# Cross-attention over 8192 context rows: feature-major context, statistics and factors through DRAM, keys and values kept in DRAM, units of 16 chunks

## The chip, the cores and the metric

The kernel runs on one core of a Trainium2 chip. The time is the device time in microseconds of one launch. The engines are PE (TensorE), DVE (VectorE), ACT (ScalarE), POOL (GpSimd) and SP (SyncE, which here only issues DMAs); each works through its own instructions in order, and semaphores tie them together. All arithmetic is in 32-bit floats.

## What is computed

A block of a perceiver: cross-attention of 512 latent tokens over 8192 context rows plus the latents themselves, then eight layers of a linear-attention transformer, then a layer of expert-choice feed-forward. The change touches the first part alone:

```
xn = layer_norm(ctx, gamma_x, beta_x)          # 8192 x 512
ln = layer_norm(latents, gamma_l, beta_l)      # 512 x 512
q  = (ln @ Wq) * 64**-0.5                      # 8 heads of 64
k_x, v_x = split(xn @ Wkv);  k_l, v_l = split(ln @ Wkv)
k_x = rope_rotate(k_x)
k, v = concat([k_x, k_l]), concat([v_x, v_l])  # 8704 rows
out = softmax(q k^T) v @ Wo
x   = x + out
```

## The kernel before

Context rows come in 16 blocks of 512 (numbers 1 to 16; block 0 holds the latents), a block in 4 chunks of 128 rows: 68 chunks in all. The eight heads form four pairs p.

**Preparing a block.** `fetch_block` loads four row tiles (128 rows x 512 features each) and the rotation table `trig`. `moments_of` takes mean and variance of each row on DVE, `roots_of` the reciprocal root on POOL for blocks after 2 (a chain of small instructions with Newton steps), `centre` subtracts and scales the rows on ACT, in place. `transpose_rows` then turns the block on PE, 16 transposes of 128x128 through PSUM, and ACT applies gamma and beta per feature on the way back (`xT`, four tiles [feature, row]). `keys_of` multiplies `xT` with Wkv for one of four groups of output features, DVE multiplies with cosine and sine, POOL adds the two halves, and eight DMAs of 64 KB on SP's queue bring the result of two groups into key tiles `k_sb[b, p]` [2 heads x 64, 512 rows] in SBUF. `values_of` gives 128 rows x 512 features, which ACT copies out of PSUM in four parts into `v_sb[b, p]`. All key and value tiles stay in SBUF until used: 27 buffers.

**Attention in units.** A unit is one pair over a run of chunks; units go round the pairs, and the number of chunks that a unit reaches grows with the blocks that are ready (`STEP = 3.25`, most units 13 chunks, 24 units). For each chunk `score` makes two 128x512 products into PSUM (five banks, `ps_s`, shared with keys, values, transposes and small helpers), ACT copies them to `sc`, and DVE keeps a running maximum `mx`. At a unit's end `maxima` transposes the running maximum on PE, reduces it on DVE to `mrow`, and forms the factor `alpha` = exp(old - new), the difference on POOL and the exponential on ACT. `maxima_rows` spreads `mrow` over PSUM (`mbc`). Then `exponentials` (DVE subtracts `mbc`, ACT takes the exponential, POOL adds into `es`) and `weigh` (PE, with the values, into `po`) run for this unit while the next unit's scores are made. `shrink` spreads `alpha` along rows by 16 small PE products into `pa` and multiplies the accumulated output `oT[p]` on DVE; `gather` adds `po` and the sum of exponentials `pd`.

**What sets the order.** The work is put into numbered steps (`at(step, function, ...)`). Each step makes the scores of two chunks and then does what is due in it, by `rank`. Block b begins at step 8(b-2); its pieces (four of keys, four of values) follow one per step, and the normalizing of block b+1 is spread over the same eight steps by `normalizing`, where the number is the offset. PE keeps the order of the code; the other engines' order is made by a scheduler when the kernel is built, with hints (`queued`, `tc.issue_after`) that hold an instruction behind another. SP issues nearly all DMAs, in one order.

Of the kernel before, what the change touches and what calls it, by code (L numbers as in the profile page):

```python
# [8 lines left out]
F32 = mybir.dt.float32  # L9
# [7 lines left out]
P = 128  # L17
# [37 lines left out]
def perceiver_kernel(  # L55
    ctx: ExitStack, tc: tile.TileContext, x, cx, wq_x, wkv_x, wo_x, wq, wk, wv, wo, wf1, wf2,
# [81 lines left out]
    xnp = pool("x_feat", 4, stack=xa)  # L138
    cbp = pool("x_rows", 4, stack=xa)
    xpool = pool("xattn", 1, stack=xa)  # L140
    kvp = pool("x_kv", 27, stack=xa)
    sp = pool("x_s", 18, stack=xa)
# [5 lines left out]
    def rows_tile(name):  # L148
        return cbp.tile([P, D], F32, tag="rows", name=name)
# [29 lines left out]
    def roots_of(b):  # L179
        eng = nc.gpsimd if b > 2 else nc.vector  # L180
        with queued(behind):
            r = rsqrt_of(mvs[b][:, :, 1], TT, 1e-5, eng)
        n = small.tile([P, TT], F32, tag="nmr", name="nmr")
        stt(eng, n, mvs[b][:, :, 0], -1.0, r, ALU.mult, ALU.mult)
        roots[b] = r, n

# [9 lines left out]
    def normalizing(b):  # L196

        yield from ((1 + t // 2, moments_of, b, t) for t in range(TT))
        yield (3, roots_of, b)
        yield from ((6 + t // 2, centre, b, t) for t in range(TT))  # L200
# [11 lines left out]
    k_sb, v_sb, xT, part, rows_of, trigs = {}, {}, {}, {}, {}, {}  # L212
# [13 lines left out]
    def keys_of(b, j):  # L226
# [21 lines left out]
        for p in (j - 1, j):  # L248
            k_sb[b, p] = kv_tile(f"k{b}_{p}")
            for h in range(2):  # L250
                src = slice((p % 2 * 2 + h) * H2, (p % 2 * 2 + h + 1) * H2)
                for i, half_of in enumerate((lo, hi)):
                    o = h * HD + i * H2
                    nc.sync.dma_start(out=k_sb[b, p][o : o + H2, :], in_=half_of[src, :])

    def values_of(b, t):
# [5 lines left out]
        for p in range(NPAIR):  # L262
            if t == 0:
                v_sb[b, p] = kv_tile(f"v{b}_{p}")
            nc.scalar.copy(v_sb[b, p][:, t * P : (t + 1) * P], pv[:, p * P : (p + 1) * P])  # L265
# [4 lines left out]
    def fetch_block(b):  # L270
        rows_of[b] = [rows_tile(f"cb{t}") for t in range(TT)]
        load_rows(
            rows_of[b], cx[(b - 1) * BLK : b * BLK, :], (nc.sync, nc.scalar) if b == 1 else (nc.sync,)
        )
        if b == 1:
            with tc.issue_after(loaded[0].ins):
                nc.scalar.dma_start(out=col, in_=cols)
            fetch_weights(0)
        trigs[b] = xpool.tile([P, 2, BLK], F32, tag="trig", name="tg", bufs=1)
# [6 lines left out]
    def fetch_last():  # L286
        wo_last.extend(rows_tile(f"wo{p}") for p in range(NPAIR))
# [20 lines left out]
    fetch_block(2)  # L308
    normalize_block(0)
# [19 lines left out]
    STEP = 3.25  # L329
    units, met, k = [], [0] * NPAIR, 0  # L330
    while min(met) < NCHUNK:
        p = k % NPAIR
        upto = min(NCHUNK, int(3 + STEP * k)) if k else 4
# [16 lines left out]
    for b in range(2, NBLK + 1):  # L350
        begin, gap = 8 * (b - 2), 1 if b < NBLK else 2

        for dc in range(DC):
            if dc == 2 and b > 2:
                at(begin, values_of, b - 1, TT - 1)
            at(begin, transpose_rows, b, dc, C_GX, C_BX)
        at(begin, *((fetch_block, b + 1) if b < NBLK else (fetch_last,)))
        pieces = *((keys_of, j) for j in range(2)), (values_of, 0), *((keys_of, j) for j in (2, 3)), (values_of, 1), (values_of, 2)
        for j, (f, i) in enumerate(pieces, 1):
# [3 lines left out]
    at(begin + 8 * gap, values_of, NBLK, TT - 1)  # L363
    pieced = set(todo)

    scores, mx, mrow, alpha, mbc, es, po = {}, {}, {}, {}, {}, {}, {}

    def score(u, i):
# [3 lines left out]
        for h in range(2):  # L372
            hs = slice(h * HD, (h + 1) * HD)
            nc.tensor.matmul(pc[h], k_sb[b, p][hs, o : o + P], qT[hs, p, :], start=True, stop=True)  # L374
# [10 lines left out]
    def maxima(u):  # L385
# [13 lines left out]
        if p in mrow:  # L399
            a = alpha[u] = small.tile([P, 2 * TT], F32, tag="alpha", name="alpha", bufs=4)  # L400
            nc.gpsimd.tensor_tensor(a, mrow[p], new, ALU.subtract)
            nc.scalar.activation(a, a, AF.Exp)
        mrow[p] = new
# [11 lines left out]
    def shrink(u):  # L415

        p = units[u][0]
        pa = bank("pa")
        for qc in range(TT):
            for h in range(2):  # L420
                c = h * TT + qc
                nc.tensor.matmul(
                    pa[h * HD : (h + 1) * HD, qc * P : (qc + 1) * P],
                    alpha[u][:, c : c + 1].to_broadcast([P, HD]), ident,
                    start=True, stop=True,
                )
# [948 lines left out]
```

## Time and profile before

| | us |
|---|---|
| median of 3 runs | 2578.23 (2577.60 to 2579.33) |
| the profiled execution, span | 2575.6 |
| PE busy in the stretch 100 to 1100 | 981 of 1000 |
| ACT, exponentials (L435) x272 | 288.3 |
| ACT, copies of scores (L377) x544 | 284.3 |
| DVE, subtraction of the maximum (L434) x272 | 319.7 |
| DVE, running maximum (L383) x448 | 283.4 |
| POOL, sums of exponentials (L445) x222 | 525.3 |

Attention runs from the first scores, at 85.5 us, to about 1236 us; the layers behind it fill the rest of the span. Some rows of the groups, with line, engine, operation, tiles, shapes and count, then the busy time in us, the mean of one in ns, and the idle time of the engine just before them with what ended it:

```profile
L246 POOL TENSOR_TENSOR cos<-cos,sin 128x512 f32<-128x512 f32 x32 | 40.9, 1280 | 0.0
L194 ACT ACTIVATE cb<-cb,nmr,ny 128x512 f32<-128x512 f32 x62 | 47.8, 838 | 4.0 <-DVE nmr L82 4.0
L224 ACT ACTIVATE xn<-pt,col 128x512 f32<-128x512 f32 x66 | 49.3, 795 | 14.0 <-PE pv L259 11.9 <-PE pt L218 1.7
L265 ACT COPY v<-pv 128x128 f32<-128x128 f32 x272 | 51.5, 275 | 37.0 <-PE pv L259 37.0
```

And from the list of DMA issues, with size and the median time from issue to landing:

```profile
k<-cos SPq DMA_DIRECT2D x272, 64.0 KB, 2.0
cb<-in_cx SPq DMA_DIRECT2D x62, 256.0 KB, 3.4
tg<-in_trig SPq DMA_DIRECT2D x16, 512.0 KB, 3.8
```

### The profile page before, as it was taken

To read this page: it belongs to the slowest core of one execution; us is meant where nothing else is said; L and a number is where in the kernel's file an instruction comes from. 1 tells how busy PE (TensorE), PEld (TensorE's weight loads), DVE (VectorE), ACT (ScalarE), POOL (GpSimd) and SP (SyncE) were. 2 spreads that over 40 slices of the span, in tenths; PEclk is the share of its full clock that TensorE was granted. 3 is DMA by queue.
4 is the path that set the end of the run, shared out by engine and by line. 5 is a ranking of instruction groups with operands and counts; after the bars stand their busy time and mean duration, and the time that the engine had idled before them with its cause. 6 is when DMAs were issued, how large, how long until landed. Compare 5 with 4: busy or idle time off the path is not lost.

```text
span 2575.6 us, 32550 instructions
## 1 busy us (share of the span) xinstructions
PE 2514.4 (98%) x10984; PEld 1490.5 (58%) x10984; DVE 1747.0 (68%) x3680; ACT 1202.9 (47%) x2285; POOL 1263.1 (49%) x1422
## 2 busy tenths in 40 slices
PE   8999999999999999997999999999999999999998
PEld 4434333334343343333588686886868868687764
DVE  4466777766677776886675766757676575766764
ACT  2465666665566666663443415334153441524303
POOL 0255665666567666675054352444525354263512
PEclk9999999999999999998999999999999999999999
DMA  4111011111111111010522223222222222222236
GB/s 136 39 45 52 27 41 42 41 41 41 33 42 41 42 41 41 9 41 17 192 94 81 84 69 116 95 94 70 95 91 94 94 86 96 93 74 98 66 113 199
DMA packets 98375, 187.41 MB, mean 73 GB/s; under 512 B 10336, under 2 KB 10464, under 8 KB 98208
## 3 DMA queue, kind: packets, MB, share of 16 engines
q1 hardware_dynamic: 88496, 167.29, 20.0%
q10 hardware_dynamic: 8688, 15.94, 1.9%
q0 software_dynamic: 1024, 2.10, 0.3%
q8 instruction: 87, 1.43, 0.2%
q14 instruction: 80, 0.66, 0.1%
HBM read 162.22 MB, written 1.05 MB: 63 GB/s over the span
## 4 chain that ended last, share of the span: by engine, by line
PE 80%; DVE 9%; ACT 5%; issue 4%; POOL 2%; DMA 0%; POOLq 0%; DVEq 0%; ACTq 0%
PE pb L839 14%; PE ps L628 13%; PE pw L723 9%; PE pv L259 7%; PE po L455 7%; PE pk L230 6%; PE pc L374 6%; PE ps L723 6%; PE po L1002 4%; DVE sc L434 4%; ACT sc L377 2%; ACT sc L435 1%; POOL es L445 1%; PE pt L218 1%; PE pf L932 1%
## 5 line engine op out<-in xcount | busy, mean ns | idle before, releaser
L445 POOL TENSOR_TENSOR es<-es,sc 128x1024 f32<-128x1024 f32 x222 | 525.3, 2366 | 111.0 <-ACT sc L435 99.9
L383 DVE TENSOR_TENSOR mx<-pc,mx 128x512 f32<-128x512 f32 x448 | 283.4, 685 | 190.7 <-ACT sc L377 190.5
L435 ACT ACTIVATE sc<-sc 128x1024 f32<-128x1024 f32 x272 | 288.3, 1064 | 242.8 <-DVE sc L434 231.7
L377 ACT COPY sc<-pc 128x512 f32<-128x512 f32 x544 | 284.3, 599 | 91.4 <-PE pc L374 78.8
L434 DVE TENSOR_TENSOR sc<-sc,mbc 128x1024 f32<-128x1024 f32 x272 | 319.7, 1211 | 3.7 <-PE mbc L411 2.2
L374 PE MATMUL pc<-qT,k 64*128 64x512 f32 x1088 | 286.1, 618 | 2.9 <-ACT v L265 1.3
L455 PE MATMUL po<-sc,v 128*64 128x512 f32 x1088 | 267.5, 612 | 0.2 <-DVE mx L383 0.2
L230 PE MATMUL pk<-xn,wkv 128*128 128x512 f32 x544 | 253.2, 609 | 7.0 <-ACT v L265 2.9
L259 PE MATMUL pv<-wkv,xn 128*128 128x512 f32 x544 | 249.6, 602 | 6.3 <-DVE sin L241 3.3
L1012 ACT ACTIVATE h<-h,col 128x256 f32<-128x256 f32 x192 | 103.9, 576 | 220.8 <-DVE h L772 151.0
L374 PEld LDWEIGHTS pc<-qT,k 64*128 64x128 f32 x1088 | 100.2, 185 | 183.2 <-issue 79.8
L896 ACT ACTIVATE g<-g 128x512 f32<-128x512 f32 x64 | 39.9, 630 | 344.7 <-DVE g L856 218.7
L230 PEld LDWEIGHTS pk<-xn,wkv 128*128 128x128 f32 x544 | 99.9, 192 | 148.9 <-issue 105.9
L259 PEld LDWEIGHTS pv<-wkv,xn 128*128 128x128 f32 x544 | 98.4, 190 | 140.7 <-issue 106.7
L723 PE MATMUL pw<-curT,cur 128*128 128x256 f32 (+1 forms) x896 | 177.4, 350 | 0.1
L805 POOL TENSOR_TENSOR sh<-h 128x128 f32<-128x128 f32 x120 | 83.4, 695 | 176.3 <-PE pb L839 171.7
L979 POOL TENSOR_TENSOR y<-qf,y 128x512 f32<-128x512 f32 x32 | 44.8, 1399 | 243.6 <-DVE y L978 243.6
L723 PEld LDWEIGHTS pw<-curT,cur 128*128 128x128 f32 x896 | 150.3, 190 | 17.0 <-DVE curT L716 0.5
L856 DVE TENSOR_TENSOR g<-g,pb 128x256 f32<-128x256 f32 x135 | 50.1, 418 | 159.7 <-PE pb L839 159.2
L455 PEld LDWEIGHTS po<-sc,v 128*64 128x64 f32 x1088 | 68.3, 138 | 147.6 <-issue 124.2
L710 POOL TENSOR_TENSOR cur<-w 128x256 f32<-128x256 f32 x128 | 93.4, 740 | 118.9 <-DVE g L897 75.2
L839 PE MATMUL pb<-tw,sh 128*128 128x256 f32 x540 | 136.1, 379 | 0.0
(220 smaller groups left out, 4643.7 us busy)
## 6 DMA issues: line engine op xcount, KB each, us to landing
w<-in_wf SPq DMA_DIRECT2D x64, 1024.0 KB, 5.3
k<-cos SPq DMA_DIRECT2D x272, 64.0 KB, 2.0
cb<-in_cx SPq DMA_DIRECT2D x62, 256.0 KB, 3.4
row<-in_rows ACTq DMA_DIRECT2D x48, 256.0 KB, 4.6
f<-in_f SPq DMA_DIRECT2D x10, 1024.0 KB, 5.4
tg<-in_trig SPq DMA_DIRECT2D x16, 512.0 KB, 3.8
wk<-in_wk SPq DMA_DIRECT2D x8, 1024.0 KB, 5.2
wq<-in_wq SPq DMA_DIRECT2D x8, 1024.0 KB, 5.2
```

Of the source, the lines that this page charges most:

```text
L230: nc.tensor.matmul(pk, wkv[:, 0, dc, j * P : (j + 1) * P], xT[b, dc], start=(dc == 0), stop=(dc == DC - 1))
L259: nc.tensor.matmul(pv, xT[b, dc][:, t * P : (t + 1) * P], wkv[:, 1, dc, :], start=(dc == 0), stop=(dc == DC - 1))
L374: nc.tensor.matmul(pc[h], k_sb[b, p][hs, o : o + P], qT[hs, p, :], start=True, stop=True)
L377: copied[0] = nc.scalar.copy(sc[:, h, :], pc[h])
L383: behind[0] = nc.vector.tensor_tensor(mx[u][:, h, :], pc[h], mx[u][:, h, :], ALU.max)
L434: nc.vector.tensor_tensor(sc, sc, mbc[u], ALU.subtract)
L435: nc.scalar.activation(sc, sc, AF.Exp)
L445: nc.gpsimd.tensor_tensor(es[u], es[u], sc, ALU.add)
L455: nc.tensor.matmul(po[u][h * HD : (h + 1) * HD, :], v_sb[b, p][:, t * P + h * HD : t * P + (h + 1) * HD], scores[u, i][:, h, :], start=(i ...
L628: nc.tensor.matmul(ps[:, t0 : t0 + n], w[:, dc, c0 : c0 + P], xT[:, dc, t0 : t0 + n], start=(dc == 0), stop=(dc == DC - 1),)
L723: nc.tensor.matmul(ps, lhs[:, k], rhs[:, k], start=(k == 0), stop=(k == 1))
L839: nc.tensor.matmul(ps[i], lhs, rhs, start=(q == 0 and i in (1, 2, 6, 5, 4)), stop=(q == self.N - 1 and i in (1, 2, 7, 3, 4)),)
```

## The change

The context is also handed in transposed (`cxt`, feature by row), so blocks 2 to 16 are loaded in the form `xT` directly, beside their rows, which now serve the statistics alone. For these blocks `roots_of` writes mean and reciprocal root into `both`, stores them in DRAM as two lines of 512 numbers, and loads each line back into all 128 partitions (`lines`); `scaled` then subtracts the mean on POOL, multiplies with the root on DVE, and applies gamma and beta on ACT. Keys and values are stored in DRAM (`k_dr`, `v_dr`) and loaded for each unit and block (`load_keys`, `load_values`) into 9 buffers in place of 27; a value piece leaves PSUM by one copy in place of four. `alpha` is stored in DRAM element by element and loaded back spread over partitions (`abc`), so that `shrink` needs no PE. Units end on block boundaries: 4, 8, 12, then 16 chunks, 20 units, and 16, 12, 8 and 4 at the end. A block's pieces begin one step earlier, the last of its values is no longer put off into the next block, and the rotation table is fetched at offset 5.

```diff
-    xnp = pool("x_feat", 4, stack=xa)
-    cbp = pool("x_rows", 4, stack=xa)
+    xnp = pool("x_feat", 2 * DC, stack=xa)
+    cbp = pool("x_rows", 2, stack=xa)
...
-    kvp = pool("x_kv", 27, stack=xa)
-    sp = pool("x_s", 18, stack=xa)
+    kvp = pool("x_kv", 9, stack=xa)
+    sp = pool("x_s", 21, stack=xa)
+    dram = pool("x_dram", 1, DRAM, stack=xa)
...
     def roots_of(b):
         eng = nc.gpsimd if b > 2 else nc.vector
         with queued(behind):
             r = rsqrt_of(mvs[b][:, :, 1], TT, 1e-5, eng)
+        if b > 1:
+            both = small.tile([P, 2, TT], F32, tag="both", name="both")
+            eng.tensor_scalar(both[:, 0, :], mvs[b][:, :, 0], 1.0, None, ALU.mult)
+            eng.tensor_scalar(both[:, 1, :], r, 1.0, None, ALU.mult)
+            line = dram.tile([2, BLK], F32, name=f"line{b}")
+            nc.sync.dma_start(out=line.rearrange("i (p t) -> p i t", t=TT), in_=both)
+            lines[b] = xpool.tile([P, 2, BLK], F32, tag="lines", name="lines")
+            nc.sync.dma_start(
+                out=lines[b], in_=line.rearrange("i n -> (i n)").partition_broadcast(P).rearrange("p (i n) -> p i n", i=2)
+            )
+            return
...
+    def scaled(b, dc):
+        xt = xT[b, dc]
+        nc.gpsimd.tensor_tensor(xt, xt, lines[b][:, 0, :], ALU.subtract)
+        with queued(behind):
+            nc.vector.tensor_tensor(xt, xt, lines[b][:, 1, :], ALU.mult)
+        with queued(copied):
+            nc.scalar.activation(
+                xt, xt, AF.Identity, bias=col[:, C_BX + dc : C_BX + dc + 1], scale=col[:, C_GX + dc : C_GX + dc + 1]
+            )
...
         yield (3, roots_of, b)
-        yield from ((6 + t // 2, centre, b, t) for t in range(TT))
+        yield from ((5 + t // 2, scaled if b > 1 else centre, b, t) for t in range(TT))
...
         for p in (j - 1, j):
-            k_sb[b, p] = kv_tile(f"k{b}_{p}")
+            k_dr[b, p] = dram.tile([P, BLK], F32, name=f"k{b}_{p}")
...
-                    nc.sync.dma_start(out=k_sb[b, p][o : o + H2, :], in_=half_of[src, :])
+                    nc.sync.dma_start(out=k_dr[b, p][o : o + H2, :], in_=half_of[src, :])
...
-        for p in range(NPAIR):
-            if t == 0:
-                v_sb[b, p] = kv_tile(f"v{b}_{p}")
-            nc.scalar.copy(v_sb[b, p][:, t * P : (t + 1) * P], pv[:, p * P : (p + 1) * P])
+        vs = tmp.tile([P, D], F32, tag="vs", name="vs", bufs=3)
+        nc.scalar.copy(vs, pv)
+        if t == 0:
+            v_dr[b] = dram.tile([TT, P, D], F32, name=f"v{b}")
+        nc.sync.dma_start(out=v_dr[b][t], in_=vs)
+
+    def load_keys(u, b):
+        kt[u, b] = kv_tile(f"kt{u}_{b}")
+        nc.sync.dma_start(out=kt[u, b], in_=k_dr[b, units[u][0]])
+
+    def load_values(u, b):
+        vt_[u, b] = kv_tile(f"vt{u}_{b}")
+        p = units[u][0]
+        nc.sync.dma_start(
+            out=vt_[u, b].rearrange("p (t f) -> p t f", t=TT),
+            in_=v_dr[b][:, :, p * P : (p + 1) * P].rearrange("t p f -> p t f"),
+        )
...
+        src = src.rearrange("(p t) d -> p t d", t=TT)
+        for i in range(2):
+            nc.sync.dma_start(out=row_pairs[f"cb{b}"][i], in_=src[:, 2 * i : 2 * i + 2, :])
+        for dc in range(DC):
+            xT[b, dc] = xnp.tile([P, BLK], F32, tag="xn", name="xn")
+            nc.sync.dma_start(out=xT[b, dc], in_=cxt[dc * P : (dc + 1) * P, (b - 1) * BLK : b * BLK])
...
-    STEP = 3.25
...
-        upto = min(NCHUNK, int(3 + STEP * k)) if k else 4
+        upto = min(NCHUNK, TT * (k + 1))
...
-        for dc in range(DC):
-            if dc == 2 and b > 2:
-                at(begin, values_of, b - 1, TT - 1)
-            at(begin, transpose_rows, b, dc, C_GX, C_BX)
         at(begin, *((fetch_block, b + 1) if b < NBLK else (fetch_last,)))
-        pieces = *((keys_of, j) for j in range(2)), (values_of, 0), *((keys_of, j) for j in (2, 3)), (values_of, 1), (values_of, 2)
-        for j, (f, i) in enumerate(pieces, 1):
+        if b < NBLK:
+            at(begin + 5, fetch_trig, b + 1)
+        pieces = *((keys_of, j) for j in range(2)), (values_of, 0), *((keys_of, j) for j in (2, 3)), *((values_of, t) for t in (1, 2, 3))
+        for j, (f, i) in enumerate(pieces):
             at(begin + j * gap, f, b, i)
...
             a = alpha[u] = small.tile([P, 2 * TT], F32, tag="alpha", name="alpha", bufs=4)
             nc.gpsimd.tensor_tensor(a, mrow[p], new, ALU.subtract)
             nc.scalar.activation(a, a, AF.Exp)
+            line = dram.tile([2 * TT, P], F32, name=f"al{u}")
+            nc.sync.dma_start(out=line.rearrange("c p -> p c"), in_=a)
+            abc[u] = xpool.tile([P, T], F32, tag="abc", name="abc")
+            for h in range(2):
+                nc.sync.dma_start(
+                    out=abc[u][h * HD : (h + 1) * HD, :],
+                    in_=line[h * TT : (h + 1) * TT, :].rearrange("c p -> (c p)").partition_broadcast(HD),
+                )
...
-        pa = bank("pa")
-        for qc in range(TT):
-            for h in range(2):
-                c = h * TT + qc
-                nc.tensor.matmul(
-                    pa[h * HD : (h + 1) * HD, qc * P : (qc + 1) * P],
-                    alpha[u][:, c : c + 1].to_broadcast([P, HD]), ident,
-                    start=True, stop=True,
-                )
         nc.vector.tensor_tensor(
-            oT[p], oT[p], pa.unsqueeze(1).to_broadcast([P, 2, T]), ALU.mult
+            oT[p], oT[p], abc[u].unsqueeze(1).to_broadcast([P, 2, T]), ALU.mult
         )
...
+        begun = end[u] + 1 - n // 2
+        for c in range(0, n, TT):
+            at(max(-1, begun + c // 2 - 3), load_keys, u, (units[u][1] + c) // TT)
...
             last = max(d + 1, first)
+            if i % TT == 0:
+                at(last - 2, load_values, u, (units[u][1] + i) // TT)
```

## The prediction

> **What bounds the kernel now.** I read the page's busy times first, then busy time in stretches, then the instruction groups up to 1250 us, then the timelines around single unit ends. The profiled execution spans 2575.6 us; the median of the runs is 2578.2 us, so 2.6 us lie around the span.
>
> ```profile
> PE 2514.4 (98%) x10984; PEld 1490.5 (58%) x10984; DVE 1747.0 (68%) x3680; ACT 1202.9 (47%) x2285; POOL 1263.1 (49%) x1422
> ```
> ```profile
> 300.00:400.00 100.00, 96.64 (x366) 37.95 (x366) 69.60 (x99) 58.53 (x106) 65.06 (x65) 1.00 0.14 39
> 1100.00:1200.00 100.00, 85.23 (x391) 35.70 (x389) 78.10 (x104) 60.08 (x97) 72.71 (x37) 0.93 0.08 27
> ```
> Columns: PE, weight loads, DVE, ACT, POOL, granted clock, DMA share, GB/s. Attention is the first half. Between 100 and 1100 us PE stands still for only 18.6 us, so work taken from PE counts nearly in full, and so does each new PE wait. Only the tail (1100 to 1250 us, 19 us idle) has another bound.
>
> ```profile
> L218 PE MATMUL pt<-ident,cb 128*128 128x128 f32 x256 | 38.1, 287 | 12.0 <-ACT cb L194 10.5 <-DVE mx L383 1.3
> L411 PE MATMUL mbc<-ident,mrow 128*128 128x128 f32 x192 | 27.8, 291 | 9.9 <-DVE sc L434 9.9
> L392 PE MATMUL pmx<-ident,mx 128*128 128x128 f32 x192 | 25.7, 275 | 1.2 <-DVE mx L383 1.2
> L494 PE MATMUL pd<-es,ones 128*64 128x512 f32 x92 | 23.7, 593 | 2.0 <-POOL es L445 2.0
> L422 PE MATMUL pa<-ident,alpha 128*64 128x128 f32 x320 | 21.8, 278 | 0.0
> ```
> **What it removes.** Context transposes: 256 take 38.1 us, but 16 of them belong to block 1, which stays (3.9 us in the timeline at 10.5 us): 34.2 us go. The alpha matmuls all go: 21.8 us. Units fall from 24 to 20: four times 25.7/24 + 27.8/24 + 23.7/23 = 3.26, so 13.0 us. Sum 69.0 us, all on PE, all in stretches where PE sets the time.
>
> **What it adds and hides.** POOL: 60 subtractions 128x512 at 1.28 us (row of L246), 77 us; DVE: 60 multiplications at 0.69, 41 us, less about 17 us for four units' reductions, factors and gathers. DVE goes from 72% towards 78%, POOL from 61% to about 70%; ACT loses 46 us (centring) and 11 us (one value copy of 0.6 us for four of 0.28). None is then the bound, so I price their volume at nothing. DMA: 17.8 MB each for value stores, key loads and value loads, 15.7 MB of feature-major context, 7.9 MB of statistics, 4.2 MB of factors: 81 MB on 47 MB in 1150 us, a share of 0.14 growing to about 0.38. A key load stands three steps (23 us) ahead of its use and 256 KB land in 3.4 us; a value load two steps. Nothing, while that cover holds; a late one costs PE the remainder.
>
> **Where the moved steps now stand.** The built order of the changed kernel, the same around each of units 4 to 14 (here unit 5), is
>
> ```
> POOL: ve, both, vh, yg, 8 small, es, 4 small, es, both | xn - lines x4 (waits the DMA of lines) | alpha (L447) | cos1, cos0 | es ...
> ACT:  4 copies sc<-pc | exp alpha (waits POOL) | 4 copies sc<-pc of the next unit | 4 exps ...
> SP:   line store | lines load (waits the store) | al store | 2 abc loads | 8 key stores ...
> PE:   pc x4, pk, pmx x8, po x4 | pc x4, mbc x8, pk, po x4 | pd, pc x4, pv ...
> ```
> Unit k ends in step 8k-5 and the roots of block k+2 are due in that same step, so for k = 4 to 14 the factor alpha stands on POOL behind a DMA round trip, and ACT, in order, cannot copy the next unit's scores out of PSUM before it. The kernel before has a milder form of this:
>
> ```profile
>   POOL alpha L401: 71.6, 17
> ```
> ```profile
> 300.22 0.22 POOL L91 TENSOR_SCALAR ve<-mvx 128x4 f32<-128x4 f32 x1
> 304.34 2.35 POOL L445 TENSOR_TENSOR es<-es,sc 128x1024 f32<-128x1024 f32 x1
> 307.07 0.21 POOL L401 TENSOR_TENSOR alpha<-mrow 128x8 f32<-128x8 f32 x1
> ```
> ```profile
> 307.31 0.21 ACT L402 ACTIVATE alpha<-alpha 128x8 f32<-128x8 f32 x1 [6.36 <-POOL alpha L401]
> 307.43 2.03 ACT L377 COPY sc<-pc 128x512 f32<-128x512 f32 x4
> ```
> ```profile
> 314.93 1.12 PE L374 MATMUL pc<-qT,k 64*128 64x512 f32 x2 [0.83 <-DVE sin L241]
> 317.26 3.70 PE L230 MATMUL pk<-xn,wkv 128*128 128x512 f32 x8 [1.21 <-DVE oT L485]
> 647.90 6.72 PE L230 MATMUL pk<-xn,wkv 128*128 128x512 f32 x8 [2.88 <-ACT v L265]
> ```
> ACT idles 71.6 us before 17 alphas; the wait of 6.36 us at 307 us cost PE 0.83 + 1.21 us, because PE works on until its five score banks are full.
>
> **The cost of that step.** Times run from the first score matmul of the unit's last step. (1) The last statistics: a step like it began at 348.0 us, its maxima ended 4.3 us later, then 1.3 + 0.2 + 1.2 + 0.1 us of statistics and one subtraction: 6.8 us into a step of 7.4, so POOL starts at -0.6. (2) 17 small operations take 4.7 us (360.05 to 364.72) and two sums 2.37 each: `both` is written at 8.8. (3) The trip through DRAM is not in the trace. Nearest: a key store lands in 2.0 us, a trig load of the same 512 KB in 3.8; I take 5.8, with 4.0 (two of the fastest) and 8.4 (two of the 4.2 us of the rows loads on ACT's queue) as ends: 14.6. (4) Four subtractions at 1.25 pitch, alpha and its exponential 0.2 each: alpha is ready at 20.0. (5) ACT ended its copies at 3.3 (349.23 + 2.05 - 348.01), so it waits 16.7 us where the longest wait before was 8.7. (6) PE works through pc 1.9, pk 3.6, pmx 1.0, po 1.9, then pc 1.9, mbc 1.0, pk 3.6, po 1.9 until 16.8, and pd finds no bank until 20.5. At 307 us the time from alpha's exponential to the first long product after it was 317.26 - 307.31 = 9.95 us, spent by ACT's copies and exponentials and DVE's subtractions, the same chain here; so the product starts at 30.0. In between pd and pc fill 2.9: idle 30.0 - 16.8 - 2.9 = 10.3 us. As a check, waits of 6.36, 6.80 and 8.70 us before cost 2.0, 1.2 and 1.3, so 4.3 to 7.4 us of a wait are covered, and 16.7 leaves 9.3 to 12.4. (7) The clock: after 2.88 us of idling at 645 us the product took 6.72 instead of 3.60 us, and the granted clock was 0.50 from 649 to 653. I take 2.0 of these 3.1 us, since part of the slow work falls where PE waits anyway; ends 0 and 3.1. Sum 12.3 per unit, eleven units: 135 us. Cheap end 9.3 - 1.8 + 0 = 7.5 (83 us), dear end 12.4 + 2.6 + 3.1 = 18.1 (199 us).
>
> The Trainium skill, "TensorE: Matmul & The Clock Gate", section "Part 1: The HAM clock gate", says that the clock halves after about one idle window of 3.4 us; the row above halves it after 2.9. An estimate from the page: a gap of 3.8 us per unit pays in full, about 1 us more for each of the eleven; it speaks against this change.
>
> The factor's own trip: al is stored element by element, 1024 pieces of 4 bytes. Nearest rows: 2.0 us (key store) and 10.9 (the 128 KB of w_c in 256-byte pieces); I take 4, nearer to the small one, then 2.0 to 3.4 for abc: ready by 27.4 and DVE, by the chain above, comes to the factor at about 30. Nothing; at 10.9, about 4 us per unit, which belongs to the dear end. The skill's page "DMA: Bandwidth & Descriptors", section "Specifications", says that pieces under 512 bytes are read, modified and written; no row here shows what that costs at 4 bytes.
>
> **What goes away of the old waits, and the tail.** In the 24 us around the sixteen alphas from 253 to 1070 us PE idles 14.3 us, and the half clock at 648 adds 3.1; two such unit ends stay as they were at 1 us each, so 15 us go into the new sum. The last units have 16, 12, 8 and 4 chunks instead of 13, 10, 7 and 4, in a stretch where DVE and POOL already hold PE up by 19 us: +3, ends -5 and +12 (four factors, each up to 3 us late).
>
> Sum: 2575.6 - 69 + 135 - 15 + 3 = 2629.6, and 2.6 around it: **2632 us**.
>
> **Rivals.** (A) *The wait is hidden*: POOL comes to alpha early enough that ACT waits no longer than now. Time 2575.6 - 69 + 3 + 2.6 = 2512. It decides below (69 + 15 - 3)/11 = 7.4 us lost per unit. For it: 4 to 7 us of a wait are covered, and the trip may be as short as 4.0. Against: the four subtractions alone are 5.0 us, and the cheap end is still 7.5. (B) *The queues hold it longer*: in five of the eleven unit ends a value load that waits for PE stands on SP between the line's store and the load of lines; if its buffer is not free, the trip grows by up to a step, 5 x 7.4 = 37: 2669. For it: SP holds 40 issues per block instead of 21. Against: nine buffers and about five in use. (C) *DVE becomes the bound*: per step it needs about 6.5 us against PE's 7.8, so no; if its in-order waits cost 1% of the stage, 11 us more. (D) The change not doing what it says: the built order has no context transposes after block 1 and no alpha matmuls, so excluded.
>
> **How the numbers follow.** Forecast 0.64, A 0.15, B (with C) 0.17, and 0.04 for losses near the 7.4 us that end level. The forecast's own range, by the ends above but not all at once, is 2590 to 2680. Taking in B's 2669 with some of the dear end, and the neighbourhood of no change, gives 2560 to 2690; A stays outside. About 0.2% (5 us) is what a measurement tells from no change: faster 0.16, same 0.03, slower 0.81.
>
> **What would show it.** Right: no pt rows after 100 us and PE's busy time near 2465 us (2514 - 69 + 22 of half clock); about eleven ACT waits for POOL's alpha of some 17 us each, 60 us or more apart; POOL idle for about 6 us on the DMA of lines before each; PE gaps of 3 us and more there with the granted clock at 0.5 after them. Wrong: alpha waits under 8 us (then A), or PE waiting for the DMA of kt or vt (then B), or PE gaps spread evenly over all steps with DVE as their releaser (then C).

## The result, and the profile after

| | us |
|---|---|
| before, median | 2578.78 (2577.60 to 2581.55) |
| after, median of 4 runs | 2720.03 (2715.63 to 2725.74) |
| ratio | 1.055, 95% interval 1.0537 to 1.0564 |
| after, the profiled execution's span | 2723.9 |

The change makes the kernel 141 us slower. The forecast had the sign and 53 us of it.

The busy times and the granted clock of the page of after:

```profile
PE 2525.3 (93%) x10344; PEld 1453.6 (53%) x10344; DVE 1809.0 (66%) x3721; ACT 1146.1 (42%) x2017; POOL 1356.6 (50%) x1482
PEclk9999899988899998889899999999999999999999
```

PE issues 640 matmuls fewer and is busy 10.9 us longer (2525.3 against 2514.4). By the rows of before, 69 us of matmul time are gone, so some 80 us of matmul time were added by a lower clock; the eights in the clock row all lie in the first half, in attention. Idle time of PE, span less busy, grew from 61.2 to 198.6 us. The two differences make up the 148.3 us by which the span grew. No other engine is near full.

The same two stretches as before (PE, weight loads, DVE, ACT, POOL, clock, DMA share, GB/s):

```profile
300.00:400.00 100.00, 83.36 (x270) 30.69 (x269) 56.16 (x82) 41.71 (x67) 60.73 (x55) 0.91 0.30 86
1100.00:1200.00 100.00, 78.32 (x245) 27.27 (x244) 62.40 (x81) 48.97 (x76) 55.93 (x30) 0.86 0.24 69
```

From 300 to 400 us PE was 96.64 us busy at clock 1.00; now it is 83.36 us at 0.91. DVE, ACT and POOL all do less per microsecond than before: nothing is saturated, everything waits in turn. For whom, the groups of PE in attention (94 to 1380 us) tell; the last part is idle time and who ended it:

```profile
L420 PE MATMUL pc<-qT,kt 64*128 64x512 f32 x1088 | 314.0, 655 | 25.6 <-DVE sin L268 19.3 <-DVE mx L429 4.8 <-ACT vs L290 1.5
L286 PE MATMUL pv<-wkv,xn 128*128 128x512 f32 x480 | 249.6, 668 | 31.8 <-ACT vs L290 25.9 <-DVE oT L530 3.0 <-DVE x_sb L530 2.9
L539 PE MATMUL pd<-es,ones 128*64 128x512 f32 x76 | 30.7, 894 | 67.7 <-ACT sc L423 62.0 <-POOL es L490 5.7
L465 PE MATMUL mbc<-ident,mrow 128*128 128x128 f32 x160 | 22.6, 286 | 9.2 <-DVE sc L479 9.2
L438 PE MATMUL pmx<-ident,mx 128*128 128x128 f32 x160 | 21.8, 278 | 3.6 <-DVE mx L429 3.6
```

The rows of `pa` and of the context transposes are gone, as the change says. The largest wait, 62.0 us ahead of `pd`, comes eleven times, and it ends when ACT has copied scores. The means show the clock: `pv` 668 ns where it was 602 before, `pd` 894 where it was 593, while `pmx` and `mbc`, which stand ahead of the gap, keep theirs (278 and 286 ns, 275 and 291 before). The row of `pv` on the page of before:

```profile
L259 PE MATMUL pv<-wkv,xn 128*128 128x512 f32 x544 | 249.6, 602 | 6.3 <-DVE sin L241 3.3
```

One unit end of after, in time (start, duration, engine, line; in brackets the idle time before and its releaser). POOL, ACT, PE and SP:

```profile
306.16 0.23 POOL L190 TENSOR_SCALAR both<-ny 128x4 f32<-128x4 f32 x1
314.10 4.92 POOL L205 TENSOR_TENSOR xn<-xn,lines 128x512 f32<-128x512 f32 x4 [7.71 <-PE po L500]
318.98 0.20 POOL L447 TENSOR_TENSOR alpha<-mrow 128x8 f32<-128x8 f32 x1
319.21 0.21 ACT L448 ACTIVATE alpha<-alpha 128x8 f32<-128x8 f32 x1 [17.91 <-POOL alpha L447]
319.45 0.36 SPq L450 DMA_DIRECT2D al<-alpha  x1
320.04 1.98 PE L539 MATMUL pd<-es,ones 128*64 128x512 f32 x4 [6.49 <-ACT sc L423]
326.84 2.07 PE L420 MATMUL pc<-qT,kt 64*128 64x512 f32 x2 [2.21 <-DVE sin L268]
328.84 6.07 PE L286 MATMUL pv<-wkv,xn 128*128 128x512 f32 x8
332.84 1.74 DVE L472 TENSOR_TENSOR oT<-oT,abc 128x1024 f32<-128x1024 f32 x1 [4.93 <-DMA abc<-al]
```

POOL has `both` ready at 306.39 and stands still for 7.71 us. The row names PE as the releaser, whose products end at 313.56; but the subtraction starts at 314.10, and the list of DMAs between 305 and 320 us shows what landed just before it (size, us from issue to landing):

```profile
lines<-line SPq DMA_DIRECT2D x1, 512.0 KB, 4.3
...
line<-both SPq DMA_DIRECT2D x1, 4.0 KB, 3.3
al<-alpha SPq DMA_DIRECT2D x1, 4.0 KB, 8.5
```

The load of `lines`, issued at 309.69, lands at 314.0. Then four subtractions, then `alpha`; ACT, which had nothing to do since 301.30, takes the exponential and can copy scores only now; PE, out of score banks since 313.55, goes on at 320.04 at about half the clock (four `pd` in 1.98 us where they took 1.03 at 311 us in before, eight `pv` in 6.07 instead of 3.60). This is the unit end with the longest trip of the eleven: POOL's idle time on the lines is 7.71 us here, between 5.83 and 7.47 at the ten others, and 6.5 on average. And then DVE waits another 4.93 us for the factor on its way through DRAM. Over the whole execution, the list of DMA issues has these medians:

```profile
al<-alpha SPq DMA_DIRECT2D x16, 4.0 KB, 9.7
...
lines<-line SPq DMA_DIRECT2D x15, 512.0 KB, 3.9
abc<-al SPq DMA_DIRECT2D x32, 128.0 KB, 4.0
```

The store of `alpha`, 4 KB in 1024 pieces of 4 bytes, takes 9.7 us, longer than the load of 512 KB. In the unit end shown 13.4 us lie between alpha's exponential (319.42) and the factor (332.84). What these waits come to for ACT and DVE, from the groups up to 1420 us:

```profile
L448 ACT ACTIVATE alpha<-alpha 128x8 f32<-128x8 f32 x16 | 3.3, 209 | 190.9 <-POOL alpha L447 190.9
L472 DVE TENSOR_TENSOR oT<-oT,abc 128x1024 f32<-128x1024 f32 x8 | 18.0, 2249 | 27.3 <-DMA abc<-al 27.3
L472 DVE TENSOR_TENSOR x_sb<-x_sb,abc 128x1024 f32<-128x1024 f32 x8 | 12.7, 1583 | 42.4 <-DMA abc<-al 42.4
L207 DVE TENSOR_TENSOR xn<-xn,lines 128x512 f32<-128x512 f32 x60 | 64.0, 1107 | 5.1 <-POOL xn L205 5.1
```

ACT idles 190.9 us ahead of `alpha` (71.6 before), DVE 69.7 us ahead of the factor (2.4 us before, for PE's `pa`). The product with the lines takes 1107 ns on average, though the shortest take 676. In the short units at the end nothing covers the factor's trip:

```profile
1189.61 1.22 DVE L472 TENSOR_TENSOR x_sb<-x_sb,abc 128x1024 f32<-128x1024 f32 x1 [10.95 <-DMA abc<-al]
1191.49 3.68 PE L500 MATMUL po<-sc,vt 128*64 128x512 f32 x8 [11.35 <-DVE x_sb L530]
```

### The profile page after: what moved, and what is told of

It is laid out like the page before. It is cut to its first block, busy times and chain, and to the rows that moved or that the text cites. A ratio compares the mean times of both kernels' runs of the same rounds, so it can differ in the third digit from the quotient of the medians.

```text
span 2723.9 us, 31724 instructions
## 1 busy us (share of the span) xinstructions
PE 2525.3 (93%) x10344; PEld 1453.6 (53%) x10344; DVE 1809.0 (66%) x3721; ACT 1146.1 (42%) x2017; POOL 1356.6 (50%) x1482
## 3 DMA queue, kind: packets, MB, share of 16 engines
q0 software_dynamic: 1024, 2.10, 0.2%
## 4 chain that ended last, share of the span: by engine, by line
PE 50%; DVE 3%; ACT 2%; issue 2%; DMA 2%; POOL 1%; SPq 0%; DVEq 0%; POOLq 0%; ACTq 0%
PE pb L889 13%; PE ps L678 12%; PE pw L773 8%; PE ps L773 6%; PE po L1052 3%; DMA al<-alpha 1%; PE pf L982 1%; POOL es L490 1%; PE pt L971 1%; PE po L500 1%; DVE sc L479 1%; PE pc L420 1%; DMA abc<-al 1%; PE pc L523 1%; ACT sc L480 0%
## 5 line engine op out<-in xcount | busy, mean ns | idle before, releaser
L490 POOL TENSOR_TENSOR es<-es,sc 128x1024 f32<-128x1024 f32 x230 | 554.2, 2409 | 187.6 <-ACT sc L480 179.1
L429 DVE TENSOR_TENSOR mx<-pc,mx 128x512 f32<-128x512 f32 x464 | 290.0, 683 | 136.9 <-ACT sc L423 136.9
L420 PE MATMUL pc<-qT,kt 64*128 64x512 f32 x1088 | 314.0, 655 | 25.6 <-DVE sin L268 19.3
L479 DVE TENSOR_TENSOR sc<-sc,mbc 128x1024 f32<-128x1024 f32 x272 | 319.1, 1207 | 0.1
L286 PE MATMUL pv<-wkv,xn 128*128 128x512 f32 x544 | 278.1, 659 | 31.8 <-ACT vs L290 25.9
L500 PE MATMUL po<-sc,vt 128*64 128x512 f32 x1088 | 268.9, 614 | 13.5 <-DVE x_sb L530 11.4
L420 PEld LDWEIGHTS pc<-qT,kt 64*128 64x128 f32 x1088 | 108.0, 197 | 228.8 <-issue 77.9
L286 PEld LDWEIGHTS pv<-wkv,xn 128*128 128x128 f32 x544 | 109.1, 210 | 201.3 <-issue 129.2
L1062 ACT ACTIVATE h<-h,col 128x256 f32<-128x256 f32 x192 | 104.0, 577 | 220.6 <-DVE h L822 150.5
L500 PEld LDWEIGHTS po<-sc,vt 128*64 128x64 f32 x1088 | 66.6, 138 | 185.6 <-issue 143.4
L427 DVE TENSOR_TENSOR mx<-pc,sc 128x512 f32<-128x512 f32 x40 | 26.0, 687 | 205.2 <-ACT sc L423 205.2
L773 PEld LDWEIGHTS pw<-curT,cur 128*128 128x128 f32 x896 | 150.2, 190 | 16.9 <-DVE curT L766 0.2
```

The lines of the kernel that those rows point to most:

```text
L286: nc.tensor.matmul(pv, xT[b, dc][:, t * P : (t + 1) * P], wkv[:, 1, dc, :], start=(dc == 0), stop=(dc == DC - 1))
L420: nc.tensor.matmul(pc[h], kt[u, b][hs, o : o + P], qT[hs, p, :], start=True, stop=True)
L429: behind[0] = nc.vector.tensor_tensor(mx[u][:, h, :], pc[h], mx[u][:, h, :], ALU.max)
L479: nc.vector.tensor_tensor(sc, sc, mbc[u], ALU.subtract)
L490: nc.gpsimd.tensor_tensor(es[u], es[u], sc, ALU.add)
L500: nc.tensor.matmul(po[u][h * HD : (h + 1) * HD, :], vt_[u, b][:, t * P + h * HD : t * P + (h + 1) * HD], scores[u, i][:, h, :], start=(i = ...
```

## The experiments

Four suspects stand in the profile of after: alpha behind the lines' trip, the factor's own trip, the feature-major context (its work on DVE and ACT), and keys and values in DRAM. All results together; "idle" is the profiled span less PE's busy time, and "unit" the mean distance of the exponentials of alpha over the ten units from the first of the eleven unit ends to the last (for kernels with units of 16 chunks):

| run | median us | ratio to before, 95% | idle | unit |
|---|---|---|---|---|
| before | 2578.78 | | 61.2 | |
| after | 2720.03 | 1.0537 to 1.0564 | 198.6 | 79.0 |
| alpha on DVE | 2635.51 | 1.0217 to 1.0248 | 150.2 | 72.5 |
| factor by PE | 2682.29 | 1.0392 to 1.0427 | 151.2 | 77.5 |
| both of these | 2546.22 | 0.9872 to 0.9902 | 86.8 | 65.6 |
| alpha ahead on POOL | 2648.91 | 1.0260 to 1.0293 | 160.6 | 72.8 |
| context as before | 2596.47 | 1.0067 to 1.0097 | 99.1 | 68.7 |
| alpha on DVE, factor later | 2574.40 | 0.9972 to 0.9996 | 105.5 | 67.5 |
| alpha on DVE, store in 32-byte pieces | 2569.83 | 0.9952 to 0.9978 | 107.0 | 67.3 |
| both, context as before | 2535.44 | 0.9815 to 0.9848 | 50.4 | 65.0 |
| before, alpha on DVE | 2557.16 | 0.9906 to 0.9933 | 50.8 | |
| both, scaling later | 2575.86 | 0.9986 to 1.0004 | 105.5 | 68.5 |
| both, product on POOL | 2518.51 | 0.9757 to 0.9784 | 65.3 | 63.4 |
| the same, start mended | 2506.71 | 0.9716 to 0.9742 | 53.3 | 63.4 |

**Alpha off POOL.** The changed kernel with one word changed:

```diff
-            nc.gpsimd.tensor_tensor(a, mrow[p], new, ALU.subtract)
+            nc.vector.tensor_tensor(a, mrow[p], new, ALU.subtract)
```

> Edit: the difference for the factor alpha is taken on DVE instead of POOL, right behind mrow; nothing else. Theory (alpha stands on POOL behind the trip of the statistics through DRAM, and ACT waits for it): ACT's waits before alpha fall from 16 to 18 us to under 3, the PE gaps of 5 to 6.6 us before pd go, the period of a unit falls from 79 us by 11 to 14, eleven times; the factor's own trip (9.7 + 4.0 us) still holds DVE by about 5 us per unit: 2600 us (2570 to 2630). Rival (the extra traffic and the longer queues slow everything): within 20 us of 2720.

2635.51 us: 85 less than the changed kernel, and just past the dear end. ACT's wait ahead of `alpha` shrinks to 54.1 us, eleven times 4.9 (under 3 were expected). What stands in its place is DVE: its waits for the factor grew, from 69.7 to 102 us (groups of that run, up to 1420 us):

```profile
L472 DVE TENSOR_TENSOR oT<-oT,abc 128x1024 f32<-128x1024 f32 x8 | 18.7, 2343 | 49.6 <-DMA abc<-al 49.6
L472 DVE TENSOR_TENSOR x_sb<-x_sb,abc 128x1024 f32<-128x1024 f32 x8 | 14.8, 1852 | 52.4 <-DMA abc<-al 52.3
```

So with alpha late, its lateness had covered part of the factor's trip; with alpha early, the trip lies open. That the step is worth as much as expected, and only shadowed by the next one, takes the run with both edits to show.

**The factor by PE again.** Alpha stays on POOL; the 16 small PE products `pa` come back, and the store and loads of the factor go:

```diff
-            line = dram.tile([2 * TT, P], F32, name=f"al{u}")
-            nc.sync.dma_start(out=line.rearrange("c p -> p c"), in_=a)
...
+        pa = bank("pa")
...
-            oT[p], oT[p], abc[u].unsqueeze(1).to_broadcast([P, 2, T]), ALU.mult
+            oT[p], oT[p], pa.unsqueeze(1).to_broadcast([P, 2, T]), ALU.mult
```

> Edit: shrink spreads alpha by PE products again, no al and abc; alpha stays on POOL. Theory: DVE's 70 us of waits for abc go, of which PE feels two thirds, 16 units get 1.1 us of PE work back; ACT's waits of 16 to 18 us stay: 2690 us (2665 to 2710). Rival (the factor's trip is the main loss): below 2640.

2682.29: 38 us less, although PE now has 256 products more, 17.5 us of work by that run's row. So the trip costs about 38 us more than the products, or 55 us before their work is taken off, even behind alpha's wait. The eleven unit ends hold 15 of the 38 (77.5 a unit for 79.0), the short units at the end 17 (from the last of the eleven alphas to the last alpha of all 203.2 us for 220.6), the rest comes after them. ACT's waits stay: 194.0 us.

**Both.**

> Edit: both of the first two (alpha's difference on DVE, the factor spread by PE). Theory: both waits go, the period of a unit is near 65 us: 2560 us (2535 to 2590), below the kernel before. Rival (traffic): above 2660. Rival (DVE is the bound): above 2600 with PE gaps ended by DVE all over.

2546.22, below the kernel before. Against the run with the factor by PE alone it differs in the place of alpha only, and in nothing that waits for a factor in DRAM: this pair is the clean measure of the step that the prediction put first. 2682.29 - 2546.22 = 136 us. The first alpha comes 12.8 us earlier, each unit of the next ten is 11.8 us shorter, and the tail is the same within 2 us. The pages of the two runs, the factor by PE alone and then both edits, tell how much of this is idle time and how much slow clock:

```profile
PE 2530.3 (94%) x10600; PEld 1468.2 (55%) x10600; DVE 1836.8 (68%) x3721; ACT 1147.5 (43%) x2017; POOL 1349.9 (50%) x1482
```
```profile
PE 2462.9 (97%) x10600; PEld 1447.5 (57%) x10600; DVE 1854.9 (73%) x3737; ACT 1149.6 (45%) x2017; POOL 1360.2 (53%) x1466
```

With the same 10600 matmuls PE is busy 67.4 us less, and idle 64.4 us less (151.2 and 86.8): half of the step's price was matmuls at a lower clock (granted on average 0.967 and 0.995). The other pair, alpha on DVE with and without the factor's trip, gives 2635.51 - 2546.22 = 89 us, again net of the products' work, for a trip that nothing covers. The two groups that carry it, in the run with both edits, up to 1420 us:

```profile
L448 ACT ACTIVATE alpha<-alpha 128x8 f32<-128x8 f32 x16 | 3.3, 206 | 54.3 <-DVE alpha L447 54.3
...
L473 DVE TENSOR_TENSOR oT<-oT,pa 128x1024 f32<-128x1024 f32 x8 | 9.7, 1207 | 0.0
```

Waits of 4.9 us ahead of alpha remain. At the first of them, at 306.87 us, PE has no idle time for 18 us on either side, as the prediction had it (4.3 to 7.4 us of a wait are covered).

**Is it POOL, or the order on POOL?** Alpha stays there, ahead of the four subtractions:

```diff
-        nc.gpsimd.tensor_tensor(xt, xt, lines[b][:, 0, :], ALU.subtract)
+        with queued(differ):
+            nc.gpsimd.tensor_tensor(xt, xt, lines[b][:, 0, :], ALU.subtract)
...
-            nc.gpsimd.tensor_tensor(a, mrow[p], new, ALU.subtract)
+            differ[0] = nc.gpsimd.tensor_tensor(a, mrow[p], new, ALU.subtract)
```

> Edit: as the changed kernel, alpha stays on POOL, but stands ahead of the four subtractions instead of behind them; the trip of the lines stays as it is. Theory (only the place behind the trip costs): ACT's waits fall from 16 to 18 us to 4 to 8, DVE's waits for abc rise as in e1: 2645 us (2615 to 2665). Rival (POOL's wait for the lines is itself what costs, through late sums or late context): above 2690.

2648.91, and ACT's wait is 65.1 us where it was 190.9 (time and times):

```profile
  POOL alpha L448: 65.1, 14
```

So 71 of the 85 us that alpha on DVE saved come from the order on POOL; the engine adds the other 13.

**Without the trip of the lines.** The context goes the way of before (transposes on PE, centring on ACT); alpha on POOL, the factor through DRAM, keys and values in DRAM and the units as in the change:

```diff
-        yield from ((5 + t // 2, scaled if b > 1 else centre, b, t) for t in range(TT))
+        yield from ((6 + t // 2, centre, b, t) for t in range(TT))
...
+        for dc in range(DC):
+            at(begin, transpose_rows, b, dc, C_GX, C_BX)
```

> Edit: context transposed on PE again and centred on ACT as in the kernel before, no feature-major loads, no lines; keys and values in DRAM, 16-chunk units and the factor through DRAM stay, alpha stays on POOL. Theory: POOL has no trip to wait for, ACT's wait before alpha falls to some 5 us, PE gets 34 us of transposes back, the late start (8 us) goes, the factor's trip stays: 2630 us (2600 to 2660). Rival (traffic of keys and values and their queue is the loss): above 2690.

2596.47, just below the expected range and 124 us less than the changed kernel, although 34 us of transposes are back on PE. ACT's wait falls to 63.6 us with alpha still behind everything else on POOL: it is the trip of the lines, with the subtractions behind it, that made alpha late.

```profile
  POOL alpha L446: 63.6, 14
```

DVE's waits for the factor stay (27.3 and 41.5 us).

**Making room for the factor, or making it fast.** With alpha on DVE, first the shrinking two steps later:

```diff
-            at(end[u] + 2, shrink, u)
+            at(min(end[u] + 4, last), shrink, u)
```

> Edit: alpha's difference on DVE as in e1, the factor still through DRAM, but its multiplication stands two steps later on DVE (step end+4, two buffers for abc). Theory (the 9.7 + 4.0 us trip costs only because DVE's order reaches the factor too early): DVE's waits for abc fall from 102 us to under 25, all of them in the last units, and PE is spared e3's 17 us of spreading: 2545 us (2525 to 2565), no more than e3's 2546 and 90 less than e1. Rival (the trip blocks SP's queue or the small pieces slow the other DMAs): above 2590.

Then, at its old place, the factor stored in the order in which it lies in SBUF, eight neighbouring numbers at a time. The factors then come back in the wrong order, so this version tells the time of the trip and is no kernel to use:

```diff
-            nc.sync.dma_start(out=line.rearrange("c p -> p c"), in_=a)
+            nc.sync.dma_start(out=line.rearrange("c p -> (c p)").rearrange("(p c) -> p c", p=P), in_=a)
```

> Edit: e1 with the factor stored in 32-byte pieces, in the order in which it lies in SBUF, so that the factors that come back are in the wrong order (the output is then not the reference's); everything else, bytes and DMAs, is the same. Theory (1024 pieces of 4 bytes make the store slow): the store lands in 2 to 3 us instead of 9.7, DVE's waits for abc fall from 102 us to under 25: 2555 us (2535 to 2585). Rival (the store is slow for another reason, such as the queue ahead of it): the store still lands after 7 us or more, 2635.

2574.40 and 2569.83, against 2635.51. In the second the store lands in 3.5 us instead of 9.7, with the same 4 KB:

```profile
al<-alpha SPq DMA_DIRECT2D x16, 4.0 KB, 3.5
```

and DVE waits 9.3 us for factors instead of 102. The first hides the trip as well (1.4 us of waits) but came out above its range. What its trace has left is DVE's product with the factor, at 2207 ns where the one with a PSUM operand takes 1207, and PE waiting 39 us for ACT's copy of values. That pointed to a third cost, which is in neither alpha nor the trip.

**What the feature-major context costs.** Both edits, and the context as before:

> Edit: e3 without the feature-major context: transposes on PE and centring on ACT as before, so that keys and values through DRAM, 16-chunk units and alpha's difference on DVE are all that is left of the change. Theory: e3 + 34 us of transposes - 5 us of the late start - some 10 us of waits for ACT's value copies: 2563 us (2545 to 2580), so keys and values in DRAM cost nothing. Rival (traffic of keys and values costs PE): above 2600.

2535.44, below its range and 11 us below the run with both edits, which has 34 us less work on PE. So, with alpha and factor out of the way, the feature-major context costs 45 us where it saves 34. The waits of the run with both edits show where to look: PE waits for ACT's value copies (`pv` 16.8 us in 14 waits), and ACT's scaling of `xn` stands ahead of those copies, waiting for DVE's product with the lines. Two rivals: the order on ACT, or the product itself. The order first:

```diff
-        nc.scalar.copy(vs, pv)
+        copied[0] = nc.scalar.copy(vs, pv)
...
+        yield from ((7, weighted, b, t) for t in range(TT) if b > 1)
```

(`weighted` is the third operation of `scaled`, on ACT.)

> The version with alpha's difference on DVE and the factor by PE products (2546), with ACT's scaling of the feature-major context put one step later, behind the copies of the values. Theory: what the feature-major context still costs there is PE waiting for ACT's value copy (21 us of idle PE) and the late start (some 5 to 8 us), both because ACT's scaling, which waits for DVE's product with the lines, stands ahead of a copy that PE needs: 2524 us (2515 to 2534), below the 2535 of the version with the context as before. Rival: it is the stretched products of DVE themselves, and moving the scaling only moves the wait to the next key product: 2538 to 2552.

2575.86: the theory fell, and the time is above its rival's range too. The waits for value copies went, and new ones came, from the waits of PE in that run (100 to 1240 us; total, times, longest):

```profile
PE pk L261 <- ACT xn L212: 20.1, 13, 2.3
PE pk L261 <- DVE sin L272: 14.8, 9, 1.8
```

The next block's key product now waits for the scaling. The product on DVE was as long as ever (1933 ns on average). Then the product itself:

```diff
-        with queued(behind):
-            nc.vector.tensor_tensor(xt, xt, lines[b][:, 1, :], ALU.mult)
+        nc.gpsimd.tensor_tensor(xt, xt, lines[b][:, 1, :], ALU.mult)
```

> The version with alpha's difference on DVE and the factor by PE products (2546), with the product of the context with its lines on POOL behind the subtraction there, instead of on DVE. Theory (order on ACT): the scaling still stands ahead of the value copies and now waits for four more POOL operations of some 1.25 us each, so PE's waits for ACT's value copies stay or grow: 2545 to 2565, although DVE sheds the 108 us that its stretched products take. Rival (the stretched products on DVE are the cost): with them gone 2520 to 2535. On either, alpha's difference, which stays on DVE with both operands in SBUF, goes on taking some 0.9 us.

2518.51, 28 us less, past the rival's cheap end: it is the product on DVE. The source view of that line, number of instructions and shortest, median and longest duration in ns, in the run with both edits:

```profile
L207 DVE TENSOR_TENSOR xn<-xn,lines x60: 678/1754/2855, 42.8 to 988.0; 128x512 f32<-128x512 f32 x60
```

and after it has moved to POOL:

```profile
L206 POOL TENSOR_TENSOR xn<-xn,lines x60: 1256/1276/1312, 44.4 to 950.1; 128x512 f32<-128x512 f32 x60
```

On DVE it takes anything from 0.68 to 2.86 us, on POOL always 1.28. In the trace of the run with both edits two such products take 3.47 us, right beside POOL's work (DVE first, then POOL):

```profile
517.99 3.47 DVE L207 TENSOR_TENSOR xn<-xn,lines 128x512 f32<-128x512 f32 x2
521.39 2.34 DVE L480 TENSOR_TENSOR sc<-sc,mbc 128x1024 f32<-128x1024 f32 x2
```
```profile
517.97 1.26 POOL L274 TENSOR_TENSOR cos<-cos,sin 128x512 f32<-128x512 f32 x1
519.19 1.73 POOL L273 TENSOR_TENSOR cos<-cos,sin 128x512 f32<-128x512 f32 x1
520.88 2.82 POOL L489 TENSOR_TENSOR es<-sc 128x1024 f32<-128x1024 f32 x1
```

while the subtraction of `mbc`, twice the size with one operand in PSUM, keeps its 1.2 us each under the same POOL. The second product, which begins at 519.71, ends at 521.46, 0.54 us after POOL's second `cos` (519.19 + 1.73 = 520.92).

**The start.** In the changed kernel the first scores come at 93.48 us instead of 85.52: the queries' products wait 5.69 us because ACT evicts the latents' transposes only after scaling block 2, which waits for its lines. On top of the last version, that scaling alone goes behind the copy of the latents' last values:

```diff
-        nc.scalar.copy(vs, pv)
+        done = nc.scalar.copy(vs, pv)
+        if b == 0:
+            copied[0] = done
```

> The version with alpha's difference on DVE, the factor by PE products and the product with the lines on POOL (2518.5), with ACT's scaling of context block 2, and of that block alone, put behind the copy of the last values of the latents. Theory: PE's idle 8.8 us before the queries' products (52.95 to 53.78 in the trace of that version: ACT evicts the latents' transposes only after the four scalings, which wait for the lines' way through DRAM) goes, and nothing later is short of block 2, as 28 us of other products stand before its first key product: 2509 us (2505 to 2513). Rival: the start is set elsewhere (loads, or the first key product of block 2), and the wait only moves: 2516 to 2521.

2506.71. The queries' products of the version without and with the edit:

```profile
53.78 15.90 PE L367 MATMUL pq<-xn,wqx 128*128 128x512 f32 x32 [8.80 <-ACT xn L250]
```
```profile
43.76 13.90 PE L369 MATMUL pq<-xn,wqx 128*128 128x512 f32 x32
```

The 8.80 us of waiting (from 44.98 to 53.78) and 2.0 us of slow clock after it are gone. This is the fastest version: 2.7% below the kernel before (0.9716 to 0.9742).

**What the kernel before had in it.** The one-word edit on the kernel before:

> The kernel before with one edit: alpha's difference is taken on DVE instead of POOL. Theory: the kernel before loses only some 15 us to exp alpha waiting behind POOL's work, so this gives 2563 us (2552 to 2572), and the rest of the gain of the run with keys and values in DRAM, units of 16 chunks and the context as before (2535) belongs to those two parts of the change. Rival: the whole gain of that run was alpha's place, and keys and values in DRAM gain nothing: 2530 to 2545.

2557.16, 20 us less: the old waits for alpha. The run with both edits and the context as before differs from this one in keys and values in DRAM, the units of 16 chunks and the small shifts of the schedule that go with them, and is 22 us faster; so that part of the change gains, and no cost of its 53 MB of extra traffic shows.

## Why the prediction was right in sign and 88 us short

**What it removes: right.** Between the kernel before with alpha on DVE and the fastest version PE's busy time falls from 2505.2 to 2451.6 us, by 53.6, at about the same clock (0.995 and 0.996); the prediction's 69 less the 17.5 of `pa`, which this version keeps, are 51.5. The times agree as well: the kernel before, less 69, less 20 for the old waits, and 17.5 for `pa`, is 2577 - 69 - 20 + 17.5 = 2505.5, and 2506.7 were measured.

**The step of alpha: right in its mechanism and its total, not in its parts.** "12.3 per unit, eleven units: 135 us" was measured as 136, with 11.8 to 12.8 a unit, by the pair that differs in this step alone. Eleven waits of ACT came, 16.0 to 17.9 us long, on average 16.7, the predicted figure. Counted as the prediction counts, from the first score product of the unit's last step (296.96), steps (2) to (6) can be read off the unit end shown, the one with the longest trip: `both` at 9.4 (said 8.8), lines there at 17.1 (14.6; the trip took 7.7 us instead of 5.8, its two DMAs 3.3 and 4.3), alpha at 22.5 (20.0), PE out of work at 16.6 (16.8), the long product at 31.9 (30.0). On average over the eleven the trip took 6.5 us. The parts are off: the prediction had 10.3 us of idling and 2.0 of slow clock in each unit, the pair has 64.4/11 = 5.9 and 67.4/11 = 6.1, in part because `pd` and `pc` already run slowly inside the stretch that the prediction counted as idle but for 2.9 us. And the version with both edits waits 16.8 us for value copies where its partner waits 4.7, so the pair may understate the step a little. That the total came within 1 us is in part luck. By the rule of the Trainium skill, "TensorE: Matmul & The Clock Gate", section "Part 1: The HAM clock gate", as the prediction weighed it, the sum would have been 1 us a unit higher, 13.3; the halving is in the trace (four `pd` in 1.98 us where 1.03 is usual, after 6.49 us of idling), but the pair stays below that sum.

**The failed step: "The factor's own trip".** The prediction took 4 us for the store of `al`, "nearer to the small one" of its two ends (2.0 and 10.9), had the factor "ready by 27.4", ahead of DVE, and wrote "Nothing". The store takes 9.7 us, near the dear end, which was the row with many small pieces; the number and size of the pieces, not the bytes, was what the nearest row had to match. The loads took 4.0, past their 3.4. In the unit end shown the factor came at 332.84 - 296.96 = 35.9 in place of 27.4. The cost is 55 us before the saved work of `pa`, 38 net, in two parts. Behind alpha's wait a unit is 1.5 us longer than with `pa`, whose own work is 1.1: 2.6 us, against the "about 4" of the dear end. In the short units at the end there is no such wait to hide behind, and PE stands still for up to 11.35 us at once; "Four factors, each up to 3 us late" was the price there. And the step was not independent of the first: net of `pa`, it costs 38 us covered by alpha's wait and 89 uncovered.

**The second failed step: "None is then the bound, so I price their volume at nothing".** DVE indeed never is the bound (66%), but the 60 products, which have both operands in SBUF, were priced at 0.69 us, which is the time of DVE's products with one operand in PSUM (`cos`, 688 ns before). Next to a busy POOL they take up to 2.9. In DVE's fixed order that delays ACT's scaling, then ACT's value copy, then PE: 28 us, in the version with both edits. Rival C named DVE's in-order waits and gave them 11 us. The place that the prediction did not look at is the start, where the lines' trip stands ahead of the latents: 12 us, measured last.

The four edits form a chain, each version differing from the one ahead of it in one place: 2720.0, 2682.3 with the factor by PE, 2546.2 with alpha on DVE too, 2518.5 with the product on POOL, 2506.7 with the start mended. Against the prediction's terms that is 55 us for nothing, 136 for 135, 28 for nothing and 12 for nothing, 96 us too little; the rest of its sum is 8 us too high (the old waits were 20 us, not 15, and the 3 us of the tail do not show), which leaves the 88. The shares belong to this order of edits. In the changed kernel itself only the 55 us were measured directly: there the first scores come 8 us late, and the product's median is 680 ns (mean 1107) against 1754 in the version with both edits, so how 28 and 12 would come out if undone first is not shown.

Rival A's time (2512) is close to what the kernel does once these four places are mended, though one of the four keeps `pa`. Rival B was wrong: PE never waits for a load of keys or values, and the lines' trip was 7.7 us at its longest, not a step longer. Of the signs that the prediction named, the ACT waits, POOL's idling on the lines and the slow clock after the gaps came; PE's busy time did not come to 2465 but to 2525, the clock's share being some 80 us where 22 were allowed.

What was not tried: whether a factor through DRAM with a store as fast but in the right order, combined with the product on POOL, would beat PE's products; alpha ahead on POOL together with the factor by PE; and why the order on POOL leaves 13 us to alpha on DVE.

## What to carry to other kernels

A small result on a detour through DRAM delays everything that stands behind it in the queue of an in-order engine: look first for the tiny instruction (here `alpha`, 0.2 us) that another engine cannot pass, and put it ahead of the wait; one changed word was worth 85 us in the changed kernel and 136 once the factor came from PE. When costing an unseen DMA, match the number and size of its pieces before its bytes. And when two late things meet in one place, the cheaper one looks free in the sum; undo each alone and both together before believing either price.

## What the runs showed of the hardware

The durations of DVE's two-operand instructions depend on where their operands lie and on what POOL does. With both in SBUF the 128x512 product takes 676 ns at the shortest and 2855 at the longest; the factor's 128x1024 product 1552 to 3276 for `oT` against 1207 on average with `pa` in PSUM; with one operand in PSUM (`mx`, `cos`, `mbc`) the rows stay at 683, 683 and 1206 ns whatever POOL does. The Trainium skill, "SBUF — State Buffer", section "Who interferes with whom", says that a DVE instruction with two inputs in SBUF contends with a GpSimd instruction that reads SBUF, and that one with at most one such input, outside the two-port modes, does not. The traces agree. The longest stretch, 2855 - 676 = 2.18 us, is just below one of POOL's sums (2.36 us), and the stretched product shown above ends 0.54 us after an instruction of POOL that was under way when it began, as if it waited for a whole one; no run tests that alone. POOL is held up less in turn: its sums take 2403 ns on average beside these products and 2365 without them, its `cos` sums 1401 and 1273.

The store in 4-byte pieces takes 9.7 us where the same 4 KB in 32-byte pieces take 3.5; the runs do not separate the number of pieces from their size.
